# Four graph layers in one fixed instruction order: branches moved to the end, the GIN features' bf16 parts written to SBUF by the node phases

## The chip, the cores and the metric

One core of a Trainium2 chip runs the kernel. Its engines are TensorE (PE in the profile, PEld for its weight loads), VectorE (DVE), ScalarE (ACT), GpSimd (POOL) and SyncE (SP, which here only issues DMAs; SPq is its queue). POOL issues the indirect DMAs, which fetch table rows by index. The metric is the device time of one execution in microseconds (us); lower is better.

## What is computed

There are N = 6250 nodes with 128 features and E = 100000 edges, sorted by destination. Two blocks follow each other, each `x = x + block(relu(layernorm(x)))`, and each block has two graph layers. Cut to what matters:

```
GINE, l = 0, 1:  agg = segment_sum(relu(x[src] + edge_attr), dst)
                 h   = (x + agg) @ W1 + b1
                 h   = relu((h - mean) * rsqrt(var + eps) * gamma + beta)
                 x   = relu(h @ W2 + b2)
GIN,  l = 0, 1:  agg = segment_sum(x[src], dst)
                 x   = relu(((1 + eps) * x + agg) @ wA.T + bA) @ wB.T + bB
                 (relu on x between the two GIN layers)
```

The mean and the variance run over all nodes, so a GINE layer's node work can't end before its last edge is summed. Every layer reads rows of all nodes by `src`, so no gather of a layer can start before the table of the layer before it is written in full.

## The kernel before

**Data.** `acc` holds 128 features x N nodes in SBUF, one column per node. A *table* in DRAM holds the node rows that the next layer gathers: table0 and table1 (f32) for GINE, table2 (f32) for GIN 0, table3 for GIN 1, whose rows are three bf16 parts (high, middle, low), 768 bytes each. `resid` in DRAM is x between the blocks. Node work goes by 13 *chunks* of 512 nodes (the last has 106).

**Edges by groups.** A group is 128 x 8 = 1024 edges; there are 98. For each group `gather` has POOL issue 8 indirect DMAs (L622), `places` makes a one-hot of the local destinations (L631, DVE), GINE adds the edge rows and takes relu (L638 DVE, L639 ACT), `sums` multiplies rows by one-hots on PE into a PSUM bank (L643), and `Columns.add` adds the bank to `acc` (L674, DVE) one group later. The buffers `g` are 8 deep in GINE, 6 or 5 in GIN.

**Counting.** The GIN layers do not gather the first 70 groups. While the GINE layers run, `Counter` counts for 280 units of 256 edges how often each source occurs for each destination (one-hots L723 and L726 on DVE, product L738 on PE, added to a window at L714; L700 clears a window on ACT, L707 stores it). The counts of 14 windows go to DRAM in 7 pairs of windows x 7 blocks = 49 *pieces* of 896 KB. In a GIN layer each piece is loaded (L883) and multiplied by the features (L891: 7 blocks x 3 bf16 parts = 21 matmuls of 512 columns). The features stand in `xp`, an SBUF tile of bf16 parts. Only groups 70 to 97 are gathered, 28 groups or 224 indirect DMAs.

**Node phases.** `Steps` runs chunks through a list of stages; each step takes every chunk that is under way one stage on, the newest first. GINE: product with W1, batch-norm statistics (L984), ACT copy (L985), and when all 13 are in, `end` (L989 to L999); then `gine_nodes`: scale (L1016), product and bias (L1025), transposes to rows (L341), and for l = 0 `store_rows` (L1006, table1). For l = 1 the rows are added to x (L1011), stored to `resid`, normalised in place by `norm` (L307 to L326, half of it on POOL) and stored to table2. After that `split` loads table2 back from DRAM and makes the three parts in `xp` for GIN 0 (L776 to L787). GIN 0's nodes make the parts in tiles `h16` (L1095 to L1103), two deep, and store them as table3; GIN 1's `load_parts` (L793) loads table3 into its own `xp`. GIN 1's last stage loads `resid` (L200), adds and stores the output.

**Order.** `in_order` fixes the order of DVE, PE and ACT to that of the program text within each layer; SP is in it only during the preparation, POOL nowhere. Between layers the scheduler is free. After each of the four edge phases stands `anew` (L968), a run-time branch on `total`: if the drawn edges fit the plan of window sizes, it is jumped over, otherwise it repeats the layer with loops that fit any input. The pools for the edge tiles (`edge`, `gine`, `gin0`, `gin1`) are opened after the preparation's pool `prep` is closed, so they take its memory.

```python
with tc.If(nc.values_load(total[0:1, 0:1], min_val=0, max_val=1) > 0):
    ...
    staged(*nodes)
```

Of the kernel before, what the change touches and what calls it, by code (L numbers as in the profile page):

```python
# [17 lines left out]
P = 128  # L18
# [75 lines left out]
def gnn_kernel(ctx: ExitStack, tc: tile.TileContext, t: dict, out: bass.AP):  # L94
# [60 lines left out]
    ps_n = psum.enter_context(tc.tile_pool(name="ps_n", bufs=1, space=bass.MemoryType.PSUM))  # L155
    small = ctx.enter_context(tc.tile_pool(name="small", bufs=3))
    work = ctx.enter_context(tc.tile_pool(name="work", bufs=3))

# [14 lines left out]
    tables = [dram.tile([N, D], F32, name=f"table{i}") for i in range(3)]  # L173
    tables.append(dram.tile([N, 3 * D], BF16, name="table3"))
# [21 lines left out]
    def load_nodes(pool, view, b0, w):  # L196

        xs = pool.tile([P, CB, D], F32, name="xs", bufs=4 if pool is work else 8)
        if w % P:
            nc.vector.memset(xs[:, w // P, :], 0.0)  # L200
        rows_io(nc.sync, view, xs, b0, w, False)
        return xs
# [12 lines left out]
    depth = [0]  # L215

    @contextmanager
    def in_order(*more_engines):


        with ExitStack() as stack:
            if not depth[0]:
                stack.enter_context(tc.manual_schedule(engines={
                    mybir.EngineType.DVE, mybir.EngineType.PE, mybir.EngineType.Activation,
                    *more_engines}))
            depth[0] += 1
            yield
            depth[0] -= 1

    first = ctx.enter_context(ExitStack())  # L230
    setup = ctx.enter_context(ExitStack())
    setup.enter_context(in_order(mybir.EngineType.SP))
# [68 lines left out]
    def norm(xs, store):  # L301
# [11 lines left out]
        def finish():  # L313
            nc.vector.reciprocal(rs[:n, 0, :nb], rs[:n, 0, :nb])
            nc.vector.scalar_tensor_tensor(rs[:n, 1, :nb], mv[:n, :nb, 0], -1.0, rs[:n, 0, :nb],
                                           op0=ALU.mult, op1=ALU.mult)
            for j in range(nb):
                bias, scale = rs[:n, 1, j : j + 1], rs[:n, 0, j : j + 1]
                if j < (nb + 1) // 2:
                    nc.scalar.activation(xs[:, j, :], xs[:, j, :], AF.Relu, bias=bias, scale=scale)  # L320
                else:
                    nc.gpsimd.tensor_scalar(xs[:, j, :], xs[:, j, :], scale, bias, op0=ALU.mult,  # L322
                                            op1=ALU.add)
            if nb > 1:
                late = xs[:, (nb + 1) // 2 :]
                nc.gpsimd.tensor_scalar_max(late, late, 0.0)  # L326
            store()
# [23 lines left out]
    def staged(*stages, over=None):  # L351

        with in_order():
            steps = Steps(stages)
            for chunk in list(chunks()) if over is None else over:
                steps.begin(chunk)
                steps.step()
            steps.end()

    class Steps:  # L360


        def __init__(self, stages):
            self.stages, self.under_way = stages, []
# [7 lines left out]
        def step(self):  # L372

            for at in reversed(self.under_way):
                at[2] = self.stages[at[1]](*at[0], at[2])
                at[1] += 1
            self.under_way = [at for at in self.under_way if at[1] < len(self.stages)]
# [33 lines left out]
    def norm_first(b, got):  # L411
# [4 lines left out]
        return norm(xs, lambda: nc.sync.dma_start(to, xs))  # L416
# [178 lines left out]
    setup.close()  # L595


    full = edge_attr[: NGF * GE].rearrange("(g p j) d -> g p (j d)", p=P, j=G)
    rest = edge_attr[NGF * GE :].rearrange("(p j) d -> p (j d)", j=G)

    def load_rows(pool, g, n):

        rows = pool.tile([P, G, D], F32, name="rows", bufs=AHEAD + 2)
        to = rows.rearrange("p g d -> p (g d)")
        if n < P:
            nc.sync.dma_start(to[:n], rest)
        elif isinstance(g, int):
            nc.sync.dma_start(to, full[g])
        else:
            nc.sync.dma_start(to, full[bass.ds(g, 1)].rearrange("o p f -> (o p) f"))  # L610
# [5 lines left out]
    def gather(pool, table, n, idx):  # L616
        if in_parts(table):
            g = pool.tile([P, G, 3 * D], BF16, name="g", bufs=5)
        else:
            g = pool.tile([P, G, D], F32, name="g", bufs=8 if pool is edge else 6)  # L620
# [60 lines left out]
    class Counter:  # L681
# [34 lines left out]
        def count(self, u):  # L716
# [30 lines left out]
            for _ in range(2 if u + 1 < a + n else len(self.chores)):  # L747
                if self.chores:
                    self.chores.pop(0)()

        def end(self):
# [3 lines left out]
            while self.chores:  # L755
                self.chores.pop(0)()

    def begin(table):

        for c, b0, n0, w in chunks():  # L760
            h = load_nodes(work, table, b0, w)
            pt = bank_a()
            for j in range(-(-w // P)):
                nc.tensor.transpose(pt[:, j * P : (j + 1) * P], h[:, j, :], ident)
            nc.scalar.copy(acc[:, n0 : n0 + w], pt[:, :w])

    def split(table, xp):


        def part(b, i):  # L770
            return xp[:, b, i * D : (i + 1) * D]

        def high(c, b0, n0, w, got):
            h = load_nodes(work, table, b0, w)[:, : -(-w // P)]
            b = slice(b0, b0 - (-w // P))
            nc.scalar.copy(part(b, 0), h)  # L776
            return h, b

        def middle(c, b0, n0, w, got):
            h, b = got  # L780
            nc.vector.tensor_tensor(h, h, part(b, 0), ALU.subtract)
            nc.scalar.copy(part(b, 1), h)
            return got

        def low(c, b0, n0, w, got):
            h, b = got
            nc.vector.tensor_tensor(part(b, 2), h, part(b, 1), ALU.subtract)  # L787

        staged(high, middle, low)

    def load_parts(table, xp):

        nc.vector.memset(xp[:, NB - 1], 0.0)  # L793
        for c, b0, n0, w in chunks():
            rows_io(nc.sync, table, xp[:, b0 : b0 - (-w // P)], b0, w, False)
# [9 lines left out]

    def gine_edges(pool, l, counter, nodes):


        table = tables[l]
        with in_order():  # L810
            if l == 0:
                begin(table)
            rows = {}
            steps, rest = Steps(nodes), list(chunks())
            cs = Columns(brow)

            half = min((a for a, _ in windows), key=lambda a: abs(2 * a - NU))
            first, last = (0, half) if l == 0 else (half, NU)
            u = first
            for s in range(NG):  # L820
                n = P if s < NGF else RP
                for r in range(s if s else 0, min(s + AHEAD + 1, NG)):
                    if r not in rows:
                        rows[r] = load_rows(pool, r, P if r < NGF else RP)
                g = gather(edge, table, n, srcs[:, s * G : (s + 1) * G])
                onehot = places(edge, table, dloc[:, s, :], plan.group(s))
                while u < last and (u - first) * (NG - 2) < (s + 1) * (last - first):
                    counter.count(u)
                    u += 1
                cs.ready(max(s - BEHIND, 0))  # L830
                cs.later(s, sums(g, n, onehot, rows.pop(s)), BEHIND)
                rows[s] = None
                steps.step()
                ready = gine_ends[rest[0][2] + rest[0][3]]
                if ready is not None and ready <= s + 1 - BEHIND:
                    steps.begin(rest.pop(0))
            counter.flush()
            while cs.late:
                cs.add(*cs.late.pop(0))
            for chunk in rest:  # L840
                steps.begin(chunk)
                steps.step()
            steps.end()
            if l:
                counter.end()
        anew(edge, table, None, pool, nodes)

    def gin_edges(pool, l, nodes):

        table = tables[2 + l]  # L850
        xp = pool.tile([P, NB, 3 * D], BF16, name="xp")
        (load_parts if in_parts(table) else split)(table, xp)
        with in_order():
            steps, rest = Steps(nodes), list(chunks())
            cs, ch = Columns(brow), Columns(hrow)
            pieces = [(c, q) for c in range(len(pairs)) for q in range(NQ)]

            own_terms = list(chunks()) if l == 0 else []
            done = 0

            def begin_nodes(s):


                c = done // NQ
                u = windows[2 * c][0] if c < len(pairs) else NU
                for chunk in list(rest):
                    end = chunk[2] + chunk[3]
                    counted, gathered = counted_ends[end], gine_ends[end]
                    by_counts = counted is not None and u >= counted
                    by_groups = gathered is not None and s >= gathered and (  # L870
# [272 lines left out]
```

## Time and profile before

| | |
|---|---|
| runs shown | 2863.62, 2867.01, 2872.32 us; median 2867.01 |
| the profiled execution | 2865.18 us; its span from first to last instruction 2863.4 us |
| busy in the span | PE 62%, DVE 48%, ACT 16%, POOL 70% |
| mean granted TensorE clock | 0.69 of full speed |
| gathers (L622, POOL) | 2016 indirect DMAs, 1950.4 us busy, mean 967 ns |
| pieces (L891, PE) | 2058 matmuls, 456.9 us |
| DMA | 421.08 MB, mean 147 GB/s |

Busy shares are averages over stages with different limits. A timeline row gives start, duration, engine, line, operation, `out<-in`, shape, how many in a row, and in brackets the idle time before it with what ended it. A table of windows gives, for each stretch of the span, each engine's busy time with its number of instructions, the granted clock, the DMA engines' busy share and GB/s. The chain of waits follows the last instruction back to what released it; here it reaches back only to 2531 us.

### The profile page before, as it was taken

The page shows a single profiled execution, that of the slowest core. Times are in us where ns is not written, and L with a number is a line of the kernel's source. Part 1 is how long each engine was busy: PE and PEld are TensorE (multiplying, and loading weights), DVE is VectorE, ACT ScalarE, POOL GpSimd, SP SyncE. Part 2 cuts the span into 40 slices and gives each one's busy share as a digit, 9 for nine tenths or more (in the row PEclk, how much of TensorE's full clock was granted, in tenths as well). Part 3 has the DMA queues.
Part 4 walks back from the last instruction along what each step waited for, and adds up shares of the span by engine and source line. Part 5 has one row for each costly group of instructions (what it writes and reads, how often), then busy time and mean ns, then how long its engine had stood idle before and what let it go on. Part 6 is the DMA issues. An engine that isn't in the chain of part 4 may idle for free. (4 is left out here: it accounts for less than half of the span.)

```text
span 2863.4 us, 28519 instructions
## 1 busy us (share of the span) xinstructions
PE 1779.2 (62%) x8163; PEld 1178.4 (41%) x8164; DVE 1368.8 (48%) x3026; ACT 457.0 (16%) x591; POOL 1996.0 (70%) x2093
## 2 busy tenths in 40 slices
PE   2444444455555554565566666566656999939998
PEld 1433333334434343444444443334434555515554
DVE  8333344444555544556576677788754111211111
ACT  2311111111211212111112111122125011110001
POOL 3777777777777764777777777777745777447772
PEclk9555555555566766555556566677778999969999
DMA  4433333334334325353454455445449666367772
GB/s 146 148 105 104 104 103 104 103 116 137 103 103 147 104 80 150 104 148 104 148 148 119 132 148 148 138 145 148 145 122 281 219 214 217 112 232 253 253 249 95
DMA packets 268394, 421.08 MB, mean 147 GB/s; under 512 B 41220, under 2 KB 196232, under 8 KB 268212
## 3 DMA queue, kind: packets, MB, share of 16 engines
q1 hardware_dynamic: 200244, 280.24, 30.9%
q0 software_dynamic: 67968, 138.78, 17.5%
q8 instruction: 70, 1.15, 0.2%
q14 instruction: 112, 0.92, 0.1%
HBM read 353.10 MB, written 65.76 MB: 146 GB/s over the span
## 5 line engine op out<-in xcount | busy, mean ns | idle before, releaser
L622 POOL DMA_INDIRECT g<-table,srcs x2016 | 1950.4, 967 | 752.3 <-issue 595.2
L643 PE MATMUL pe<-onehot,g 128*128 128x120 f32 (+24 forms) x4256 | 801.4, 364 | 798.9 <-ACT g L639 793.7
L643 PEld LDWEIGHTS pe<-onehot,g 128*128 128x128 f32 (+1 forms) x3584 | 719.6, 303 | 914.1 <-ACT g L639 906.6
L638 DVE TENSOR_TENSOR g<-g,rows 128x1024 f32<-128x1024 f32 x196 | 239.9, 1224 | 635.8 <-DMA g<-table,srcs 628.2
L891 PE MATMUL pa<-piece,xp 128*128 128x512 f16 x2058 | 456.9, 381 | 47.0 <-DMA piece<-counts 42.9
L738 PE MATMUL pa<-at_j,lo_j 128*128 128x450 f16 (+22 forms) x1172 | 385.8, 475 | 117.7 <-DVE win L714 85.9
L639 ACT ACTIVATE g<-g 128x1024 f32<-128x1024 f32 x196 | 207.1, 1057 | 1562.8 <-DVE g L638 1259.0
L726 DVE TENSOR_SCALAR at_j<-numbers,code 128x1470 f16<-128x1470 f16 (+13 forms) x560 | 362.7, 648 | 0.0
L714 DVE TENSOR_TENSOR win<-win,pa 128x450 f32 (+17 forms) x586 | 313.9, 574 | 80.3 <-PE pa L738 68.8
L891 PEld LDWEIGHTS <-xp 128*128 128x128 bf16 x2058 | 201.6, 98 | 291.6 <-issue 63.5
L738 PEld LDWEIGHTS <-lo_j 128*128 128x128 f16 x1172 | 161.3, 144 | 294.7 <-issue 144.6
L631 DVE TENSOR_TENSOR onehot<-numbers,dloc 128x896 f32<-128x896 f32 (+23 forms) x252 | 224.4, 890 | 11.6 <-issue 6.8
L674 DVE TENSOR_TENSOR acc<-acc,pe 128x112 f32 (+18 forms) x252 | 60.6, 241 | 249.6 <-PE pe L643 116.9
L723 DVE TENSOR_SCALAR lo_j<-numbers,slo 128x128 f16<-128x128 f16 x560 | 153.4, 274 | 2.3 <-issue 2.3
L700 ACT COPY win<-zero 128x1001 f32<-128x1001 f32 x98 | 94.0, 1018 | 34.4 <-DVE zero L1055 34.4
L984 DVE BATCH_NORM_STATS2 bst<-pn 128x6 f32<-128x512 f32 (+1 forms) x26 | 17.3, 666 | 144.5 <-PE pn L333 144.5
L1078 ACT ACTIVATE y<-pn,vcols 128x512 f32<-128x512 f32 (+1 forms) x26 | 17.2, 661 | 431.4 <-PE pn L333 431.4
L674 DVE TENSOR_TENSOR acc<-acc,pa 128x256 f32 x28 | 11.8, 421 | 102.4 <-PE pa L891 101.9
L333 PE MATMUL pe<-y,L_gnn_W 128*128 128x512 f32 (+1 forms) x52 | 33.2, 736 | 30.4 <-ACT y L1016 24.5
L1096 DVE TENSOR_TENSOR h<-pn,h 128x512 f32<-128x512 f32 (+1 forms) x13 | 8.6, 660 | 75.5 <-ACT h L1095 75.5
L322 POOL TENSOR_SCALAR xs<-xs,rs 128x128 f32<-128x128 f32 x24 | 12.0, 510 | 46.2 <-ACT rs L311 30.2
L333 PE MATMUL pn<-acc,L_gnn_W 128*128 128x512 f32 (+1 forms) x52 | 41.9, 902 | 3.5 <-ACT acc L985 2.8
(163 smaller groups left out, 594.5 us busy)
## 6 DMA issues: line engine op xcount, KB each, us to landing
rows<-in_edge_attr SPq DMA_DIRECT2D x194, 512.0 KB
piece<-counts SPq DMA_DIRECT2D x98, 896.0 KB
counts<-win SPq DMA_DIRECT2D x98, 448.0 KB
g<-table,srcs POOLq DMA_INDIRECT x2016
xs<-table SPq DMA_DIRECT2D x24, 256.0 KB
table<-h SPq DMA_DIRECT2D x12, 384.0 KB
xp<-table SPq DMA_DIRECT2D x12, 384.0 KB
x_first<-in_x SPq DMA_DIRECT2D x8, 384.0 KB
```

Of the source, the lines that this page charges most:

```text
L333: nc.tensor.matmul(p[:, :w], w_t, rhs, start=True, stop=True)
L622: nc.gpsimd.indirect_dma_start(out=g[:n, j, :], out_offset=None, in_=table, in_offset=bass.IndirectOffsetOnAxis(ap=idx[:n, j : j + 1], axi ...
L631: nc.vector.tensor_tensor(onehot, cols[:, None, :w].to_broadcast([P, G, w]), dl[:, :, None].to_broadcast([P, G, w]), ALU.is_equal)
L638: nc.vector.tensor_add(g[:n], g[:n], rows[:n])
L639: nc.scalar.activation(g[:n], g[:n], AF.Relu)
L643: nc.tensor.matmul(pe, g[:n, j, f : f + D], onehot[:n, j, :], start=(j, f) == terms[0], stop=(j, f) == terms[-1])
L700: self.chores.append(lambda v=flat[:, q * n : (q + 1) * n], n=n: nc.scalar.copy(v, self.zero.to_broadcast([P, n])))
L714: nc.vector.tensor_add(v, v, pa[:, : n * w].rearrange("p (b w) -> p b w", w=w))
L723: nc.vector.tensor_scalar(lo_j, cols16[:, MID : MID + P], slo[:, col : col + 1], None, op0=ALU.is_equal)
L726: nc.vector.tensor_scalar(at_j[:, :width], cols16[:, :width], code[:, col : col + 1], None, op0=ALU.is_equal)
L738: nc.tensor.matmul(pa[:, : n * w], los[j], ats[j][:, b * w : (b + n) * w], start=j == 0, stop=j == UT - 1)
L891: nc.tensor.matmul(pa, xp[:, q * QB + b, i * D : (i + 1) * D], v[:, :, b, :], start=q + b + i == 0, stop=q == NQ - 1 and b == QB - 1 and i ...
```

## The change

- One `in_order` context holds everything up to the end of GIN 1, and it now holds POOL and SP as well as DVE, PE and ACT. All five engines run in the order of the program text.
- The branches are gone from between the layers. `total` is loaded once into a register (`unplanned`, in GINE 0's fourth group), and one `tc.If` at the very end computes all four layers anew (`general`, with its own tables).
- The pool `edge` (tiles `g` and `onehot` of the GINE layers) is opened before the preparation, so it no longer takes the preparation's memory.
- `own_terms` (was `begin`, table0 to `acc`) uses the one-deep PSUM bank `pn` instead of the three-deep `pa`; `xs` is 5 deep.
- GINE 1's edge rows are loaded ahead from within GINE 0's last groups. Counting is spread over NG - 6 groups instead of NG - 2, two more chores (clears, stores) are done per group, and the last window is stored within the group loop.
- `gine_nodes` has the bias as a stage of its own. For l = 1 eight stages follow each other: scale, product, bias, transposes, `normalized` (add x, store resid, statistics), `scaled_rows` (all of the scaling on POOL, into a new tile `h`), and two stages that make the parts directly in `xps[0]`, the last of which stores table2. Table2 now has 768-byte rows of bf16 parts; `split` and its loads are gone.
- GIN 0's nodes write their parts straight into `xps[1]` and store table3 from there; `h16` and `load_parts` are gone. Both `xp` tiles live in one pool `gin`.
- The pieces of the first two pairs are ordered by block, and as soon as a block's chunks have their parts, GINE 1's node phase issues one piece per step. The rest follows in the GIN loop. Piece tiles are 4 deep (were 5), loaded up to three ahead over the layer's end; gathers in GIN have 4 buffers (were 6 and 5).
- GIN 1 loads `resid` in its first node stage instead of its last.

The core of the diff:

```diff
-    def in_order(*more_engines):
...
+    def in_order():
+
+        return tc.manual_schedule(engines={
+            mybir.EngineType.DVE, mybir.EngineType.PE, mybir.EngineType.Activation,
+            mybir.EngineType.SP, mybir.EngineType.Pool})
...
+    gine_pools = ctx.enter_context(ExitStack())
     small = ctx.enter_context(tc.tile_pool(name="small", bufs=3))
     work = ctx.enter_context(tc.tile_pool(name="work", bufs=3))
+    edge = gine_pools.enter_context(tc.tile_pool(name="edge", bufs=1))
...
+    def parts_stages(xp, table):
+
+        def part(b0, n, b, i):
+            return xp[:n, b0 + b.start : b0 + b.stop, i * D : (i + 1) * D]
+
+        def high(c, b0, n0, w, h):
+            for n, b in parts_of(w):
+                nc.scalar.activation(part(b0, n, b, 0), h[:n, b, :], AF.Relu)
+                nc.vector.scalar_tensor_tensor(h[:n, b, :], h[:n, b, :], 0.0, part(b0, n, b, 0),
+                                               op0=ALU.max, op1=ALU.subtract)
+            return h
+
+        def others(c, b0, n0, w, h):
+            for n, b in parts_of(w):
+                nc.scalar.copy(part(b0, n, b, 1), h[:n, b, :])
+                nc.vector.tensor_tensor(part(b0, n, b, 2), h[:n, b, :], part(b0, n, b, 1),
+                                        ALU.subtract)
+            rows_io(nc.sync, table, xp[:, b0 : b0 - (-w // P)], b0, w, True)
...
+    two = min(2, len(pairs))
+    order = [(c, q) for q in range(NQ) for c in range(two)]
+    order += [(c, q) for c in range(two, len(pairs)) for q in range(NQ)]
...
+        def load(self):
+
+            for k in queue[self.l * len(order) + self.done :][:4]:
+                if k not in tiles:
+                    _, c, q = k
+                    flat = gin.tile([P, QB * 2 * WC], F16, name="piece", bufs=4)
+                    flat = flat[:, : pairs[c] * QB * WC]
+                    nc.sync.dma_start(flat, counts[c][:, q].rearrange("p n b w -> p (n b w)"))
...
+    steps = Steps((*gine_nodes(1, *end()), normalized, scaled_rows, *parts_stages(xps[0], tables[2])))
+    for chunk in chunks():
+        steps.begin(chunk)
+        behind = set(steps.done)
+        steps.step()
+        if products[0].ready(behind):
+            products[0].piece()
+    while steps.under_way:
...
+    with tc.If(unplanned > 0):
+        general()
```

## The prediction

> **What bounds the kernel now.** I read the busy times by stage first, cutting the span where POOL's row of gathers stops and starts (columns: stretch, its length, busy time and instructions of PE, PE's loads, DVE, ACT, POOL, granted clock, DMA share, GB/s).
>
> ```profile
> 67.00:1061.00 994.00, 485.63 (x1995) 387.40 (x1993) 442.71 (x1018) 141.35 (x149) 755.38 (x784) 0.56 0.39 112
> 1061.00:1107.00 46.00, 26.80 (x103) 15.71 (x103) 17.05 (x38) 18.95 (x30) 0.49 (x1) 0.74 0.67 200
> 1107.00:2115.00 1008.00, 603.99 (x2366) 411.66 (x2366) 689.21 (x1280) 173.45 (x178) 768.85 (x784) 0.62 0.45 132
> 2115.00:2191.00 76.00, 40.12 (x140) 21.62 (x141) 39.49 (x166) 37.75 (x80) 22.45 (x38) 0.70 0.84 239
> 2191.00:2491.00 300.00, 295.71 (x1635) 168.49 (x1634) 60.60 (x96) 41.56 (x71) 213.23 (x224) 0.99 0.65 209
> 2491.00:2558.00 67.00, 15.82 (x46) 8.88 (x47) 10.01 (x17) 12.32 (x23) 19.88 (x21) 0.60 0.50 157
> 2558.00:2849.00 291.00, 288.82 (x1787) 151.17 (x1785) 49.67 (x78) 15.77 (x23) 191.89 (x203) 0.99 0.69 230
> ```
>
> The two GINE layers hold 784 gathers each: 994/784 = 1.27 us and 1008/784 = 1.29 us, a gather of 0.94 us plus 0.30 us of issue. POOL's stream sets their pace. In the two GIN layers PE is busy 99%, and the gathers need only 280 us of the 291 to 311. Between these four stretches lie gaps of 67, 46, 76 and 67 us. Next I read POOL's waits, which price these gaps (total, times, longest):
>
> ```profile
> POOL g L622 <- issue: 595.2, 1953, 0.3
> POOL g L622 <- DVE xp L793: 59.8, 1, 59.8
> POOL g L622 <- DMA table<-h: 46.0, 1, 46.0
> POOL xs L322 <- ACT rs L311: 30.2, 1, 30.2
> POOL g L622 <- PE pa L585: 27.1, 1, 27.1
> ```
>
> No wait but these exceeds 15 us. The change leaves the streams alone, so I cost the gaps, one by one, from timeline rows:
>
> ```profile
> 40.01 0.26 SPq L416 DMA_DIRECT2D table<-x_last  x1
> ...
> 66.63 1.17 POOL L622 DMA_INDIRECT g<-table,srcs  x1 [27.07 <-PE pa L585]
> ...
> 1079.88 0.29 ACT L991 ACTIVATE bn<-bmv,eps_bn 128x1 f32<-128x1 f32 x1 [5.31 <-ACTq L968]
> ...
> 2519.30 0.58 ACT L1095 CAST h<-pn 128x512 bf16<-128x512 f32 x1 [4.75 <-DMA table<-h]
> ...
> 2531.67 13.82 SPq L194 DMA_DIRECT2D xp<-table  x13
> 2545.54 91.16 SPq L883 DMA_DIRECT2D piece<-counts  x20
> ...
> 2557.86 2.72 PE L891 MATMUL pa<-piece,xp 128*128 128x512 f16 x6 [42.91 <-DMA piece<-counts]
> ...
> 2857.96 0.29 DVE L1011 TENSOR_TENSOR xs<-xs,pn 106x128 f32<-106x128 f32 x1 [4.43 <-DMA xs<-resid]
> ```
>
> **1. Start.** Table0 is issued by 40.27 us and the sources are ready long before, yet gathering starts at 66.63: its tiles lie in the preparation's memory. With `edge` opened first, the first gather waits for table0 alone. Last table store to first gather took 3.9 us at the next boundary (1103.62 to 1107.50), so it starts at 44.2: **-22.4**, and POOL carries that through GINE 0. Cover: eight `g` tiles last until 44.2 + 8 x 10.15 = 125. Their first reader, `sums`, ran at 97.0. It gets later: `own_terms` in one bank goes PE 0.63, ACT 0.58 and two hand-overs of 0.25, some 1.7 us a chunk, from 79.6 (ACT clears windows until then) to 102, where three banks ended at 91.4. SP now issues the edge rows behind the own-term loads. First sums at about 106, still 19 us of cover; afterwards DVE needs 3 to 5 us a group against 10. Ends: -26 (no landing time) and 0.
>
> A row speaks against it: beside DVE's 1.22 us add at 2100.68 a gather took 1.98 instead of 0.94. Were all 18 early gathers so hit, 19 us of the 22.4 would go; beside a DVE busy 68% (GINE 1) the mean was 0.98, which costs under 1. I take the mean. [...]
>
> **2. GINE 0 to 1.** ACT's square root stood 5.31 us at the branch, 4.1 of it after its input was ready (1075.8). DVE waited 1.0 there, and counting work between the batch-norm steps made them 0.9 longer than at the second boundary (1.95 against 1.01). Gone: 6.0. Added: one stage, a step of 1.3. Net **-5** (ends -7, 0). What is late next is the chain of 13 chunks at 1.3 us, unchanged.
>
> **3. GINE 1 to GIN 0**, the disputed one. Batch norm is ready at 2130.7, now 0.9 earlier. Removed: 13 reloads by `split`, the in-place normalising's waits on `resid` stores, the late `x` loads. Added: pieces inside the node steps. A full step is DVE 0.6 + 0.8 + 0.3 + 0.3 + 0.6 + 0.6 = 3.2 us, and some 0.7 of waiting for ACT between: 3.9. First row add at 2135, steps 4 to 8 take 15, so the first block is ready at 2150. SP, now in program order, issues the piece loads only there, behind the step's stores. Issue to use took 12.3 us behind thirteen other loads; I take 8: first piece at 2158.
>
> ```profile
> 2179.51 6.35 PE L891 MATMUL pa<-piece,xp 128*128 128x512 f16 x21 [4.14 <-DMA resid<-xs]
> ...
> 2197.07 4.70 PE L891 MATMUL pa<-piece,xp 128*128 128x512 f16 x21
> ```
>
> The first is slow, the next take 4.53; a step on PE is 4.53 + 0.86 + 0.44 = 5.8, longer than DVE's. The last chunk's transposes stand behind six pieces: 2158 + 7.7 + 5 x 5.8 = 2195; its short chain 6, the store 3.9: 2205. Until then x 3.2, resid 3.2, table2 4.8 and ten pieces 9.2 MB must move: 20.4 MB in 75 us, 272 GB/s, where the busiest slice shows 281 at a DMA share of 0.9. I add 5: gathering starts at **2210, 19 later** than now. Given back in GIN 0: 11 pieces (50 us) are done, sums fall from 16 f32 matmuls (1.95 us) to 24 bf16 (1.18 to 1.6, GIN 1's rows). PE has 43 x 4.53 + 39 + 9 + 20 = 263 us left from 2196, so the 28 groups are now bound by POOL: 281.3 of issue, 1.7 landing, 1.3 sums: 2494.3 where the last sums now end at 2497.6. Net **-3.3**. Ends: -23 (gathers at 2190, as now) and +26 (every piece cold: seven steps of 9.4, gathers at 2239).
>
> Now PE has gaps of some 2 us a group. Row: after 2.93 us idle the sums at 2493.89 ran at half speed (3.74 us for 16). If every gap did that, PE's room of 35 us would be used up, and 5 to 10 us more, inside the upper end. [...]
>
> **4. GIN 0 to 1.** From the last sums PE needs 17.3 us for the remaining chunks (2497.63 to 2514.94), as before. Then it waited for thirteen loads of `xp` and a piece queued behind them, until 2557.86. Both now stand in SBUF, the pieces loaded ahead: the first three (15.7) end at +33.0. ACT's waits for `h16` stores (4.75 + 3.53) are gone: last part at +20, table3 stored and gathering at +23.9 (now +34.4), first group landed at +35.6, PE's stall 2.6. First sums +35.6 instead of +75.9: -40.3 for PE. But POOL moves only by 10.5, and its last group (2811.8 - 10.5 + 1.7 + 1.3 = 2804.3) replaces PE (2841.6) as the end: **-37.3**. Ends: -25 (store and clock slow) and -41.
>
> **5. End.** The last add waited 4.43 us for `resid`, now loaded two stages earlier: **-4.6** (2857.96 to 2853.4). The one branch left stands where the fourth one stood: 0, at worst 5.8, what the branch before L793 cost DVE.
>
> **Sum:** -22.4 - 5 - 3.3 - 37.3 - 4.6 = -72.6 on the profiled execution's 2865.2, which lies 1.8 below the median of the runs shown: 2794 in median terms.
>
> **Rivals.**
> - *The node phase runs clean* (term 3 at its low end, loads fast enough): 2794 - 20 = 2774. For: the old gap, with reloads, was 76 us; against: DMA share 0.84 in it.
> - *The node phase is bound by PE and DMA* (term 3 at +26): 2823. For: the piece at 6.35 us, 281 GB/s. Against: PE is continuously fed there.
> - *The early gathers don't do what they are moved for*, held by DVE or an unseen wait: 2816.
> - *SP's fixed order starves PE*: slower than before. A chunk's store waits for DVE at the end of a step, and the next piece load stands behind it on SP, some 6.5 us late. Three pieces ahead give 13.6 us of cover, leaving 7.1. If landing takes the 12.3 us seen once, each of some 22 stores inside the GIN loops costs 5.2: +114, **2908**. It decides from 72.6/22 = 3.3 us a store, a landing of 10.4 us. Against: from 2573 to 2838 PE never waited for a piece, at 230 GB/s, and the 12.3 stood behind thirteen loads.
>
> **Chances.** Forecast 0.50, spread 2781 to 2808; clean 0.17; bound 0.17; early gathers lost 0.08; starved 0.06; a mild starving that lands near the old time 0.02. About 0.3% (8.6 us) is what a measurement can tell from no change, so faster 0.92, same 0.02, slower 0.06. The range takes in the clean case and the bound one: 2768 to 2836.
>
> **What would show it.** First gather near 44, the last of GINE 0 near 1039 (term 1). About 41 us between GINE's streams (2). Batch norm ready to GIN 0's first gather near 80 us, POOL without pauses in GIN 0 and PE busy some 0.9 (3). PE idle under 5 us between GIN 0's last transposes and the first piece (4). No wait on `resid` at the end (5). Waits of L985 on `piece` inside the GIN loops, or POOL waiting for free `g` tiles, would make the prediction wrong.

## The result and the profile after

| | us |
|---|---|
| before, median of 4 runs | 2868.19 (2863.62 to 2872.32) |
| changed, median of 4 runs | 2824.16 (2823.01 to 2827.79) |
| ratio | 0.985, 95% interval 0.983 to 0.987 |
| forecast | 2794, range 2768 to 2836 |

The change gains 44 us; the forecast's terms add up to 72.6, and its 2794 lies 74 under this median. The changed kernel's profiled execution took 2827.79 us with a span of 2826.0, 3.6 over its median. Its busy times, cut where POOL's gathers stop and start and at the last sums of both GIN layers (columns as before):

```profile
44.60:1047.60 1003.00, 500.68 (x2023) 392.76 (x2023) 463.96 (x1147) 142.25 (x149) 764.32 (x784) 0.87 0.39 114
1047.60:1091.00 43.40, 29.54 (x103) 14.95 (x103) 17.49 (x38) 19.47 (x30) 0.05 (x1) 0.74 0.34 95
1091.00:2097.50 1006.50, 603.75 (x2368) 409.82 (x2366) 691.54 (x1284) 173.55 (x178) 767.79 (x784) 0.63 0.47 139
2097.50:2206.30 108.80, 80.34 (x331) 39.34 (x332) 46.86 (x179) 36.18 (x69) 31.01 (x50) 0.81 0.66 212
2206.30:2490.00 283.70, 252.98 (x1686) 138.25 (x1685) 54.96 (x85) 36.34 (x57) 213.57 (x224) 0.95 0.66 212
2490.00:2516.10 26.10, 20.83 (x75) 9.13 (x75) 6.13 (x11) 11.12 (x21) 0.00 (x0) 0.85 0.42 133
2516.10:2807.40 291.30, 278.20 (x1731) 146.28 (x1730) 50.43 (x77) 12.38 (x18) 212.25 (x224) 0.98 0.71 231
```

PE now has room in GIN 0 (252.98 of 283.70) and almost none in GIN 1 (278.20 of 291.30). Put beside the old span, stretch by stretch, this is the whole account ("batch norm" is the end of its last instruction before GINE 1's scaling; both columns add up to the spans, up to rounding):

| stretch, us | before | changed | forecast |
|---|---|---|---|
| start to first gather | 66.6 | 44.6 | 44.2 |
| GINE 0, first to last gather | 994.9 | 1003.1 | 994.8 |
| GINE 0 to 1, no gather | 46.0 | 43.4 | 41 |
| GINE 1, first to last gather | 1007.7 | 1006.5 | unchanged |
| last gather to batch norm | 15.5 | 14.8 | 0.9 less |
| batch norm to GIN 0's first gather | 60.2 | 94.0 | 80 |
| GIN 0, first gather to last sums | 306.7 | 283.7 | 284.3 |
| last sums to GIN 1's first gather | 34.4 | 26.1 | 23.9 |
| GIN 1, first gather to last sums | 309.6 | 291.3 | 282.8 |
| last sums to the end | 21.8 | 18.6 | 17.2 |

Three rows carry most of what is missing: 14 us in the node phase ahead of GIN 0, 8.5 in GIN 1, 8 in GINE 0. POOL's waits (total, times, longest) show the start and the three boundaries that are left, and no other long one before a gather. The releaser that they name is the one that came last by the profile; what these gathers need is the table.

```profile
POOL g L616 <- PE pa L732: 47.6, 15, 43.4
POOL g L616 <- DMA piece<-counts: 47.3, 2, 28.3
...
POOL g L616 <- DMA vrows<-in_L_gnn_b1b: 4.9, 1, 4.9
```

Four timeline rows answer to those of before: the first gather, the square root that stood at the branch, the first pieces of GIN 1, the last add of `resid`.

```profile
44.58 1.17 POOL L616 DMA_INDIRECT g<-table,srcs  x1 [4.93 <-DMA vrows<-in_L_gnn_b1b]
...
1061.08 0.29 ACT L784 ACTIVATE bn<-bmv,eps_bn 128x1 f32<-128x1 f32 x1 [0.29 <-DVE bmv L782]
...
2506.51 13.76 PE L985 MATMUL pa<-piece,xp 128*128 128x512 f16 x63
...
2818.39 0.29 DVE L804 TENSOR_TENSOR xs<-xs,pn 106x128 f32<-106x128 f32 x1 [0.67 <-DMA xs<-resid]
```

Their waits fell from 27.07, 5.31, 42.91 and 4.43 us to 4.93, 0.29, nothing and 0.67. Each wait that the change was to remove is gone, so the missing time lies in what came late next. The end of GINE 1's node phase, on PE, DVE, SP's queue and POOL:

```profile
2132.74 0.15 PEld L985 LDWEIGHTS <-xp 128*128 128x128 bf16 x1
...
2138.84 0.68 DVE L804 TENSOR_TENSOR xs<-xs,pn 128x512 f32<-128x512 f32 x1
...
2140.39 0.50 SPq L199 DMA_DIRECT2D table<-xp  x1
2140.94 2.36 SPq L963 DMA_DIRECT2D piece<-counts  x4
...
2147.75 7.28 PE L985 MATMUL pa<-piece,xp 128*128 128x512 f16 x21 [14.59 <-DMA piece<-counts]
...
2156.36 0.69 DVE L804 TENSOR_TENSOR xs<-xs,pn 128x512 f32<-128x512 f32 x1 [13.46 <-PE pn L339]
...
2187.33 0.33 SPq L963 DMA_DIRECT2D piece<-counts  x1
...
2188.98 0.88 DVE L852 TENSOR_TENSOR xp<-h,xp 128x512 bf16<-128x512 f32 x2
...
2191.86 0.33 SPq L963 DMA_DIRECT2D piece<-counts  x1
2192.28 0.41 SPq L199 DMA_DIRECT2D table<-xp  x1
2196.39 0.33 SPq L963 DMA_DIRECT2D piece<-counts  x1
2196.81 0.26 SPq L199 DMA_DIRECT2D table<-xp  x1
...
2206.35 1.02 POOL L616 DMA_INDIRECT g<-table,srcs  x1 [19.04 <-DMA piece<-counts]
```

The last parts stand in SBUF at 2189.9 (L852). Their store is issued only at 2196.81: SP goes in program order, and the piece loads ahead of it (L963) wait until PE has released a piece tile, once in 4.5 us. From that store to the first gather 9.5 us pass, where the runs 1 to 3 below, with no load in front of it, need 6.4 to 6.6: here an 896 KB piece was issued 0.42 us before it.

The first piece had waited 14.59 us for its own load. PE began to read its features at 2132.74, but SP issued the load only at 2140.94, behind that step's store. As PE's order is fixed, the node work behind the piece stood too: DVE's row adds (L804), otherwise 4.0 us apart, are here 17.5 us apart. So 13.5 us of the phase are this one wait. In GIN 1, PE waits for gathered rows again, which was not forecast:

```profile
2520.77 0.61 PE L637 MATMUL pe<-onehot,g 128*128 128x112 bf16 x6 [0.50 <-DMA g<-table,srcs]
...
2525.33 1.62 PE L637 MATMUL pe<-onehot,g 128*128 128x112 bf16 x12 [3.44 <-DMA g<-table,srcs]
...
2527.83 6.71 PE L985 MATMUL pa<-piece,xp 128*128 128x512 f16 x21
...
2552.91 9.23 PE L985 MATMUL pa<-piece,xp 128*128 128x512 f16 x42
```

After these waits a piece takes 6.71 us, at a granted clock of 0.69; later two take 9.23, at 1.00. From 2540 on PE has no pause, and the last sums end at 2807.4, 11.0 after POOL's last gather ended.

### The profile page after: what moved, and what is told of

It reads as the page before. It is cut to its first block, busy times and chain, and to the rows that moved or that the text cites. A ratio compares the mean times of both kernels' runs of the same rounds, so it can differ in the third digit from the quotient of the medians.

```text
span 2826.0 us, 28703 instructions
## 1 busy us (share of the span) xinstructions
PE 1786.2 (63%) x8387; PEld 1160.4 (41%) x8388; DVE 1371.4 (49%) x3026; ACT 450.1 (16%) x566; POOL 2012.6 (71%) x2106
## 5 line engine op out<-in xcount | busy, mean ns | idle before, releaser
L637 PE MATMUL pe<-onehot,g 128*128 128x16 f32 (+25 forms) x4480 | 790.7, 350 | 810.4 <-ACT g L633 767.8
L637 PEld LDWEIGHTS pe<-onehot,g 128*128 128x128 f32 x3136 | 657.7, 317 | 881.9 <-ACT g L633 881.8
L985 PE MATMUL pa<-piece,xp 128*128 128x512 f16 x2058 | 466.7, 386 | 14.6 <-DMA piece<-counts 14.6
L732 PE MATMUL pa<-at_j,lo_j 128*128 128x450 f16 (+22 forms) x1172 | 397.0, 486 | 111.2 <-DVE win L708 77.7
L625 DVE TENSOR_TENSOR onehot<-numbers,dloc 128x896 bf16<-128x896 f32 (+23 forms) x252 | 224.5, 891 | 10.0 <-issue 10.0
L637 PEld LDWEIGHTS <-g 128*128 128x128 bf16 (+1 forms) x1344 | 81.8, 99 | 62.9 <-DMA g<-table,srcs 42.5
L867 ACT ACTIVATE y<-pn,vcols 128x512 f32<-128x512 f32 (+1 forms) x26 | 17.2, 661 | 380.5 <-PE pn L331 380.5
L319 POOL TENSOR_SCALAR h<-xs,rs 128x128 f32<-128x128 f32 x49 | 31.0, 646 | 58.8 <-ACT rs L308 31.2
L804 DVE TENSOR_TENSOR xs<-xs,pn 128x512 f32<-128x512 f32 (+1 forms) x26 | 17.0, 654 | 87.6 <-PE pn L339 86.9
L1038 DVE TENSOR_TENSOR h<-pn,xp 128x512 f32<-128x512 f32 (+1 forms) x13 | 8.6, 660 | 87.3 <-ACT xp L1037 87.3
```

Source lines behind the costliest of these rows:

```text
L625: nc.vector.tensor_tensor(onehot, cols[:, None, :w].to_broadcast([P, G, w]), dl[:, :, None].to_broadcast([P, G, w]), ALU.is_equal)
L637: nc.tensor.matmul(pe, g[:n, j, f : f + D], onehot[:n, j, :], start=(j, f) == terms[0], stop=(j, f) == terms[-1])
L732: nc.tensor.matmul(pa[:, : n * w], los[j], ats[j][:, b * w : (b + n) * w], start=j == 0, stop=j == UT - 1)
L985: nc.tensor.matmul(pa, xp[:, q * QB + b, i * D : (i + 1) * D], v[:, :, b, :], start=q + b + i == 0, stop=q == NQ - 1 and b == QB - 1 and i ...
```

## The experiments

**Theory.** The pieces put into the node phase hurt it twice, by PE's time in its steps and by their loads on SP; GIN 1 is bound by PE, because its first groups have too few pieces to fill the wait for the first rows. **Rivals.** The node phase is bound by DVE and by its transfers anyway; GIN 1 ends by POOL, as forecast. All edits are to the changed kernel. Each ratio is to the kernel before, run on the same chip beside it (changed kernel: 0.985). Where the runs 1 to 4 ran, the kernel before took 2860.2 us, 8 less than above, so their totals are held against the expected ones by ratio.

**1. Four pieces in the node phase,** loaded before it.

```diff
-            self.load()
+            if more:
+                self.load()
...
+    products[0].load()
     for chunk in chunks():
...
-        if products[0].ready(behind):
-            products[0].piece()
+        if products[0].done < 4 and products[0].ready(behind):
+            products[0].piece(more=False)
...
+    products[0].load()
```

> Edit to the changed kernel: four pieces are loaded ahead of GINE 1's node phase, only these four are multiplied inside it, and no piece is loaded before its last table2 store. Theory (the pieces themselves made this phase late): their 4.5 to 7.3 us on PE stretch its steps from the 4.0 us that DVE needs to 5.0 to 5.8, and the last table2 store, whose rows were ready at 2189.9, stood on SP behind piece loads until 2196.8 and then took 9.5 us to the first gather where a store at the GINE boundary took 4.6. Then batch norm to first gather falls from 94.0 to about 72 (7 to the first row add, 13 steps of 4.0, 8 for the last chunk's stages, 5 for store and landing), GIN 0 stays bound by POOL at 284, and the total falls by 18 to 22 from 2824 to 2802 to 2806. Rival A (DVE's steps and the 20 MB of transfers set this phase, the pieces lie beside them): batch norm to first gather stays within 4 us of 94, total 2820 to 2826. Rival B (the pieces not done here bind PE in GIN 0): the gathers start 20 us earlier, but the stretch from them to the last sums grows from 284 to 300 or more, total 2816 to 2826.

2790.8 us, ratio 0.975 (0.973 to 0.978): by ratio some 28 us less than the changed kernel, where 18 to 22 were expected. Batch norm to first gather, then first gather to last sums, in its table of windows, and its first piece, which waits for nothing:

```profile
2102.23:2169.30 67.07, 40.16 (x159) 19.75 (x160) 42.69 (x168) 33.90 (x65) 30.72 (x50) 0.78 0.63 197
2169.30:2453.29 283.99, 276.17 (x1837) 150.70 (x1837) 55.04 (x85) 36.28 (x57) 212.12 (x224) 0.98 0.71 238
...
2122.99 6.31 PE L986 MATMUL pa<-piece,xp 128*128 128x512 f16 x21
```

The phase takes 67 us, where 72 were expected instead of 94, and GIN 0 still 284: PE works 23 us more there, within POOL's time. Both rivals fall. The seven other early pieces bought GIN 0 nothing. The edit changes three things at once: fewer pieces, the first loads ahead of the phase, and no load before the last store. Run 3 and the rows part them.

**2. No piece in the node phase.**

```diff
     for chunk in chunks():
         steps.begin(chunk)
-        behind = set(steps.done)
         steps.step()
-        if products[0].ready(behind):
-            products[0].piece()
...
+    steps.end()
```

> Edit to the changed kernel: no piece inside GINE 1's node phase; all 49 pieces of GIN 0 come in its gather loop. Theory: batch norm to first gather as with four pieces, about 72 us instead of 94; GIN 0 becomes bound by PE, 49 pieces of 4.6, 28 sums of 1.45 and some 30 us of node work, 296 us instead of 284; total some 10 us under the changed kernel's, 2812 to 2816. Rival A (DVE and transfers set the node phase): first gather where it was, GIN 0 12 us longer, total 2834 to 2840. Rival B (the 11 pieces done early are worth their full 50 us to GIN 0): GIN 0 grows by 40 or more, total 2845 or more.

2799.7 us, ratio 0.979 (0.976 to 0.981).

```profile
2101.90:2166.45 64.55, 22.82 (x75) 11.31 (x76) 42.46 (x168) 33.46 (x65) 30.72 (x50) 0.71 0.59 180
2166.45:2463.60 297.15, 292.02 (x1921) 158.59 (x1921) 55.24 (x85) 36.16 (x57) 212.69 (x224) 0.99 0.71 241
```

The phase is only 2.5 us shorter than with four pieces, and GIN 0 is bound by PE at 297, as expected. So of none, four and eleven pieces four are best: they cost 2.5 us early and save 13 later. Numbers between weren't tried.

**3. No piece loads behind the last chunk's start.**

```diff
     while steps.under_way:
...
-        if products[0].ready(behind):
-            products[0].piece()
+        if products[0].ready(behind) and queue[products[0].done] in tiles:
+            products[0].piece(more=False)
+    products[0].load()
```

> Edit to the changed kernel: after GINE 1's last chunk has begun, no more pieces are loaded; those already loaded are multiplied, and the next loads follow behind the last table2 store. Theory: the last 12 us of the phase are a queue on SP and in the DMA rings, the last store waiting 7 us for piece loads that wait for PE, and landing 5 us late behind them: the first gather comes at batch norm plus 82 to 86 instead of 94, steps before that stay 5.0 to 5.8, total 2813 to 2818. Rival (PE's pieces alone, not the queue, make the last rows late): the first gather within 4 us of where it was, total 2820 to 2826.

2805.7 us, ratio 0.981 (0.979 to 0.983); batch norm to first gather 84.8 us, as expected. Two row adds of DVE that follow each other, then the last store and the first gather:

```profile
2127.92 0.67 DVE L804 TENSOR_TENSOR xs<-xs,pn 128x512 f32<-128x512 f32 x1
2147.01 0.69 DVE L804 TENSOR_TENSOR xs<-xs,pn 128x512 f32<-128x512 f32 x1 [15.03 <-PE pn L339]
...
2180.78 0.39 SPq L199 DMA_DIRECT2D table<-xp  x1
...
2187.26 1.01 POOL L616 DMA_INDIRECT g<-table,srcs  x1 [9.33 <-DMA piece<-counts]
```

This parts the 27 us. From the last row add (L804) to the first gather 13.8 us pass, as with four pieces (13.9), instead of 23.6: SP's queue is worth 9.7, of which 6.7 lie before the store's issue and 3.1 behind it. From the first row add to the last it takes 64.9 us, as in the changed kernel (63.4), where four pieces need 45.9. Of the changed kernel's 17.5 us more, 13.5 are the wait for the first piece's load, which stands in run 3 too (19.1 us between the two adds shown). Only 4.0 are left for the other pieces' time on PE. So some 23 of the 27 us come from where the loads stand in SP's order, and only 4 from PE's time, which the theory had put first. The first loads put ahead of the phase with all eleven pieces kept were not tried by themselves.

**4. Six pieces before GIN 1's first sums.**

```diff
-            pieces_to(start + max(3, -(-(s - KG + 1) * (len(order) - start) // (NG - KG - 1))))
+            pieces_to(start + max(6 if l else 3, -(-(s - KG + 1) * (len(order) - start) // (NG - KG - 1))))
```

> Edit to the changed kernel: GIN 1 multiplies six pieces instead of three before its first sums. Theory: GIN 1 is bound by PE after all; PE stood 8.5 us for first gathers between 2520.8 and 2539.8 and ran the pieces there 5 us slower; with six pieces in front these waits go, and the last sums end 7 to 10 us earlier, where POOL's 280 us bind; total 2814 to 2818. Rival (POOL's stream sets GIN 1's end, as forecast): no change, 2822 to 2826.

2815.5 us, ratio 0.985 (0.982 to 0.987): no change from the changed kernel's ratio; GIN 1 took 290.3 us from first gather to last sums. The expectation failed by its edit:

```profile
2494.46 27.36 PE L985 MATMUL pa<-piece,xp 128*128 128x512 f16 x126
2521.66 2.23 PE L637 MATMUL pe<-onehot,g 128*128 128x112 bf16 x42
2526.68 1.03 PE L637 MATMUL pe<-onehot,g 128*128 128x112 bf16 x9 [2.79 <-DMA g<-table,srcs]
```

With six in front, the schedule has no piece left between the sums of the next groups: PE does 42 of them at once and waits there instead, 12.5 us in all against 11.3.

**5 to 8** ran on a chip on which the kernel before too was slower: 3389.2 us, 18% more. The changed kernel itself did not run there, so only differences between these four count.

**5. Three pieces ahead throughout GIN 1.**

```diff
-            pieces_to(start + max(3, -(-(s - KG + 1) * (len(order) - start) // (NG - KG - 1))))
+            pieces_to(start + max(3, 3 * l - (-(s - KG + 1) * (len(order) - start) // (NG - KG - 1))))
```

> Edit to the changed kernel: in GIN 1 every group has three more pieces ahead of it than before (5, 7, 9, ... instead of 3, 4, 6, ...). Theory: GIN 1 is bound by PE, which stood 11.3 us for gathered rows, nearly all of it in the first three groups; six pieces first alone did not help, since the groups behind them then had none between their sums and PE waited there. With two pieces in every gap, 9.2 + 1.4 us against POOL's 10.15 a group, PE never waits, the pieces end some two groups before the gathers, and POOL's last group ends the layer: last sums at first gather plus 283 instead of 291, total 7 to 9 us under the changed kernel. Rival (PE has no idle time that counts, or piece loads can't follow): under 3 us.

3322.1 us, ratio 0.980 (0.979 to 0.982). GIN 1 took 343.9 us from first gather to last sums; in the three runs beside it 355.1, 355.2 and 355.5. PE's waits for gathered rows are gone. The stage gains 11 us, where 8 were expected. The median total lies 8.3 us under run 8's and 3.5 under run 7's, which has a gain of its own. The stage's gain shows again in run 11.

**6. The edge pool opened after the preparation.**

```diff
-    edge = gine_pools.enter_context(tc.tile_pool(name="edge", bufs=1))
...
+    edge = gine_pools.enter_context(tc.tile_pool(name="edge", bufs=1))
     gine = gine_pools.enter_context(tc.tile_pool(name="gine", bufs=1))
```

> Edit to the changed kernel: the pool of the edge tiles is opened after the preparation again, as in the kernel before. Theory: first gather at 66.6 instead of 44.6, GINE 0's stream of 784 gathers stays between 993 and 1003 us, as in the runs so far, and all that follows comes 22 us later: total +20 to +23. [...] Rival B (an unseen wait takes the early start back): total within 5 us of the changed kernel.

3343.9 us, ratio 0.987 (0.985 to 0.989), 13.5 us over run 8. The first gather came at 66.6, but GINE 0 ended only 11 to 16 us later than beside it. That is close to the numbers of run 10's rival (collisions with DVE), but the rows show another cause. On this chip the first sums are so late (155.2 in run 5) that all eight `g` tiles are full. POOL's stops, in run 5 with the early pool and in run 6 with the late one:

```profile
159.56 0.94 POOL L616 DMA_INDIRECT g<-table,srcs  x1 [34.94 <-issue]
...
169.76 0.94 POOL L615 DMA_INDIRECT g<-table,srcs  x1 [23.32 <-issue]
```

The stop is 11.6 us longer with the early pool. The cover that the prediction counted as 19 us is exceeded here, and 6 to 11 us of the gain go with it. Run 10 repeats the edit elsewhere.

**7. The counter's last products added before each node phase** (as before the change).

```diff
+        counter.flush()
         if l:
             ahead[:] = chunks()
```

> Edit to the changed kernel: the counter's last products are added to the window before each GINE layer's node phase, as the kernel before did. Theory: the two PSUM banks of the last counted unit stay taken through the node phase, so that the transposes of GINE 0's nodes have one bank, and each waits 0.75 us for DVE's copy of the chunk before: steps of 1.44 us. With all three banks the steps fall to ACT's 1.30 and the last ones to 0.9: last gather of GINE 0 to first of GINE 1 from 43.4 to 40 to 42 us; the total, 1 to 3 us less, is too small to tell from no change. Rival (the additional stage itself makes the step longer): 43.4 stays.

3325.6 us, ratio 0.980 (0.978 to 0.981). DVE's copies of table1's rows now follow each other every 1.30 us, every 1.44 in run 8 beside it, as in the changed kernel:

```profile
1070.24 0.69 DVE L799 COPY h<-pa 128x512 f32<-128x512 f32 x1 [0.75 <-PE pa L339]
...
1071.68 0.69 DVE L799 COPY h<-pa 128x512 f32<-128x512 f32 x1 [0.75 <-PE pa L339]
```

The gap between GINE's layers is 67.5 us against 72.2 and 72.4 in runs 8 and 5, but 61.0 in run 6, so that here only the steps count. In run 11 the gap is 41.3, against 43.5 and 43.3 beside it. The rival falls: it is not the added stage but the products left standing. By the program these hold two of the three PSUM banks that the transposes use; the profile doesn't name the holder.

**8 and 12. No piece of GIN 1 loaded before GIN 0's nodes are done.**

```diff
-            for k in queue[self.l * len(order) + self.done :][:4]:
+            for k in queue[self.l * len(order) + self.done : (self.l + 1) * len(order)][:4]:
```

> Edit to the changed kernel: no piece of GIN 1 is loaded before GIN 0's nodes are done; the first loads follow table3's last store on SP. Theory (GIN 1's start is bound by its first gathers, not by pieces): the first piece moves from 2506.5 to about 2517 of the changed kernel's time, but PE then waited 11 us for gathers within its first three groups, and these waits take the delay up: last sums and total within 2 us; the first gather may come 1 us earlier, with no piece load beside table3's stores. Rival (the forecast's reason, PE's stall for pieces is what the layer's end pays for): total +9 to +11.

> The edit of the run without load-ahead once more, on another chip, read by stages: GIN 0's last sums to GIN 1's last sums took 315.7 to 317.4 us in four profiles with load-ahead. Theory (waits for GIN 1's first gathers take the delay up): first piece 9 to 11 us later, the stretch within 2 us of these. Rival (PE's stall for pieces is paid at the layer's end): 325 or more.

Run 8: 3330.4 us, ratio 0.983 (0.981 to 0.986), last sums to last sums 381.6 us against 380.6 and 381.2 in runs 6 and 7. Run 12, on another chip, a single execution: 2822.3 us, where the kernel before took 2861.3.

```profile
2511.56 16.16 PE L985 MATMUL pa<-piece,xp 128*128 128x512 f16 x63 [10.73 <-DMA piece<-counts]
2527.56 1.34 PE L637 MATMUL pe<-onehot,g 128*128 128x112 bf16 x24
```

The first piece waits 10.73 us, but now all 24 products of the first sums run without a wait, and last sums to last sums is 317.3, where the runs 1 to 4, 9 and 10 with load-ahead have 315.3 to 317.4. Loading pieces across the layer's end is worth nothing as placed. What remains as the gain of this boundary, by before's rows, is that no thirteen loads of `xp` stand ahead of the pieces; that was not undone by itself.

**9, 10 and 11** ran together: the changed kernel, the late edge pool, and the edits of 1, 5 and 7 in one.

> The changed kernel itself once more, without an edit, as the measure for the two runs beside it. Expected: a ratio to the kernel before of 0.983 to 0.987, as measured; GINE 0's stream between 993 and 1003 us, since its 1003 in the changed kernel's profile would be one execution's chance (the same instructions took 994 to 996 in four runs on another chip).

> The same edit as in the run of the late edge pool, on a chip of its own speed. Theory: against the changed kernel beside it the first gather comes 22 us later, GINE 0's stream keeps its length within 5 us, total +17 to +23. Rival (collisions with DVE take part of the early start back): stream shorter by 7 or more, total +15 or less.

> The changed kernel with four pieces in the node phase, three more pieces ahead in GIN 1, and the counter's products added before each node phase. Theory: the gains add, since they lie in different stretches: batch norm to first gather 67 instead of 94, GIN 0 stays at 284, GIN 1 from first gather to last sums 283 instead of 291, GINE 0 to 1 in 40 to 42 instead of 43.4; total 34 to 40 us under the changed kernel, a ratio to the kernel before of 0.971 to 0.973. Rival (with the pieces shifted, GIN 1's loads or PE bind elsewhere): only the node phase's 27 and flush's 2, ratio 0.974 or more.

| | us | ratio | GINE 0 | batch norm to gather | GIN 1 |
|---|---|---|---|---|---|
| 9, changed | 2819.8 | 0.983 (0.981 to 0.985) | 998.5 | 93.8 | 289.7 |
| 10, edge late | 2842.3 | 0.991 (0.989 to 0.993) | 997.8 | 93.4 | 289.6 |
| 11, three edits | 2786.1 | 0.971 (0.970 to 0.973) | 1001.2 | 66.4 | 281.8 |

Run 10: 22.5 us over run 9, first gather 22.1 later, the stream 0.7 shorter. The early pool pays in full. Run 11 is 33.8 under the changed kernel, just short of the 34 to 40 expected and above the rival's 29; the gains add. Its GIN stages, in the order first gather to last sums of GIN 0, boundary, first gather to last sums of GIN 1:

```profile
2177.24:2460.75 283.51, 276.13 (x1837) 150.70 (x1837) 55.00 (x85) 36.31 (x57) 212.73 (x224) 0.98 0.72 239
2460.75:2486.72 25.97, 20.71 (x75) 9.03 (x75) 6.14 (x11) 11.12 (x21) 0.00 (x0) 0.86 0.42 134
2486.72:2768.53 281.81, 275.62 (x1737) 145.74 (x1735) 50.05 (x77) 14.44 (x21) 211.75 (x224) 0.99 0.74 240
```

Both layers now end by POOL, with PE busy 276 us of 282 to 284: in GIN 1 the last sums end 2.1 us after the last gather, where they took 11.0.

## Why the prediction was right in sign and 30 us off

1. **Start: right.** 44.6 for 44.2, and run 10 prices it at 22.5 for 22.4. The row set against it, a gather of 1.98 us beside DVE's add, counts for little here: the 17 gathers of these 22 us, beside a DVE busy 20.1, took 17.30 us in all, 1.2 more than at 0.95 each. The sign "the last of GINE 0 near 1039" failed, as the stream took 8.2 us longer than before. In it the 784 gathers keep POOL busy 764.3 us instead of 755.4, and 25 of them take over 1.2 us instead of 13, most of these beside DVE's row adds (15 against 8) and one-hots (9 against 5). The same loops of GINE 0 took 994.6 to 1001.2 us in runs 1 to 4, 9, 11 and 12, so some of the 8 us is the chance of one execution; what sets it each time is not shown.
2. **GINE 0 to 1: half.** The branch's stall went, as costed. "Added: one stage, a step of 1.3" missed that every step became 1.44, since `flush` no longer ran at the layer's end (run 7); with it the gap is 41.3, the forecast's 41.
3. **GINE 1 to GIN 0: the mechanism right, its size wrong, within its ends.** GIN 0's length came out as worked out (283.7 for 284.3, bound by POOL), and the granted clock, for which PE's gaps were feared, was 0.95 in it. The first gather came 94 us after batch norm, not 80. "I take 8: first piece at 2158", 28 us after batch norm, was 35: the loads were issued 28.6 us after batch norm instead of 20, only 2 of this from a later first row add, while from issue to use they took 6.8 instead of 8. That the node work stands still for this first load (13.5 us here) is in the forecast's times too, unnamed. The stretch "its short chain 6, the store 3.9" and 5 for bandwidth, 15 in all from the last transposes, was 23.9: the last rows stood 6.9 us in SBUF behind SP's piece loads, for which the sum has no term, while the 9.5 us from the store to the gather are near the 3.9 and 5. So SP's fixed order, the very rival that was put on the loops inside GIN, acted at this boundary (run 3). The prediction had PE at 263 us of work under POOL's 281, but didn't ask how many of the eleven early pieces that takes: four are enough (runs 1 and 2). The rival that had PE and DMA bind this phase gives 2823, near the result, but by a first gather 109 us after batch norm; that it came out so near is luck, as three smaller losses made the same total.
4. **GIN 0 to 1: the step that failed is "its last group ... replaces PE (2841.6) as the end".** PE came free for pieces at once, as forecast, and gathering began 26.1 us after the last sums (23.9). But the pieces then ran out of place: PE stood 11.3 us for rows and was slow behind these pauses (6.71 us for the piece shown), so GIN 1 still ended by PE, 8.5 us later than forecast. Runs 5 and 11 give this back. Run 12 shows that the piece loads ahead, part of the forecast's reason, count for nothing as placed.
5. **End: near.** Last sums to last add fell from 16.6 to 11.3 us, as costed; from there to the end it is 7.3 instead of 5.2. Whether the one branch left is the cause wasn't tried; from the last sums to the end, runs 1 to 4, 9, 10 and 12 spread from 17.8 to 20.5 us.

The starving rival did not appear where it was placed: apart from the 14.59 us shown, PE never waits for a piece. On the clock, two windows of the changed kernel at the end of GIN 0, where PE pauses for 2.11 and 1.68 us with 0.37 us of work between:

```profile
2477.28:2480.70 3.42, 0.49 (x5) 0.18 (x3) 0.35 (x2) 0.00 (x0) 2.53 (x3) 1.00 0.90 336
2480.70:2484.10 3.40, 1.79 (x10) 1.51 (x11) 0.09 (x1) 0.59 (x1) 2.76 (x3) 0.50 0.31 83
```

The granted clock falls from 1.00 to 0.50 at 2480.70, within the second pause. Each pause is shorter than the 2.93 us of the prediction's row, and the 3.42 us before the fall were not empty: PE was busy 0.49 us in them. In this trace each clock holds for 3.41 us or a multiple of it, but for the last, which ends with the trace. The clock falls 90 times, and PE was busy for 63% or less of the 3.41 us before each fall (23% in the mean). Of the 207 stretches of 3.41 us at full clock that no fall follows, the least busy had PE busy for 44%. The two ranges overlap, so these counts give no limit; but one long pause was not needed, as 38 of the 90 falls come without a pause of 3 us.

## What to carry to other kernels

Work moved into another engine's phase pays only as far as it takes that engine out of the bound of the next stage; count how much is needed, and move no more. In a fixed order, look for each store that others wait for and name what stands before it on its queue: a load waiting for a free tile holds up the store behind it (6.9 us before GIN 0). Do the same for the first load of a new kind of work, as an engine that stands for it holds up all that follows in its order (13.5 us here). When a stall is removed, ask whether the bound engine has work for every remaining wait, group by group; a total that fits doesn't show that.

## What the runs showed of the hardware

Runs 5 to 8 show how much one chip can differ: in run 6, PE stood 282.6 + 102.8 + 69.6 = 455 us in waits that the profile calls issue, ahead of sums, counting and pieces.

```profile
PE pe L636 <- issue: 282.6, 113, 23.6
...
PE pa L731 <- issue: 102.8, 60, 18.5
PE pa L985 <- issue: 69.6, 66, 2.9
```

The same program's waits of run 10 have none among their longest. They are not 455 us of lost time: in run 10 PE stands 788.9 us for ACT's rows ahead of the same sums, in run 6 only 238.2. What delays the instructions there was not tried. The ratios of the four edits there (0.980 to 0.987) stay near those on the other chips, though the early pool's gain shrank.
